# A state-space layer and a routed feed-forward on one core: the scan's sum as one bf16 product, and the round's steps moved to other chunks

## The chip, the core and the metric

The kernel runs on one NeuronCore of a Trainium2 chip. The core has a tensor engine (PE in the profile; its weight loads are listed apart as PEld), a vector engine (DVE), a scalar engine (ACT), GpSimd (POOL) and a sync engine (SP) that issues transfers. Each engine runs its own instructions in their program order and waits for the others by semaphores. The metric is the device time of the whole kernel in microseconds, lower is better. Before the change the median of three runs is 478.21 us (477.84 to 479.93).

## What is computed

A sequence of 4096 tokens with 256 values goes through two layers, each followed by adding its input and a layer norm. The first is a selective state-space layer, the second a feed-forward of eight experts, of which each token uses one:

```python
xz = input_tensor @ W_in                        # 256 -> 1024: conv_in, gated
y = causal_conv4(conv_in) + conv_b              # per channel, 512 channels
convolved = silu(y)
x_dbl = convolved @ W_x                         # 33 columns: delta, B (16), C (16)
delta = softplus(x_dbl[..., :1])
h = exp(delta * A) * h + delta * B * convolved[..., :16]     # step by step, 16 states
ssm_out = sum(h * C, axis=-1)                   # one number per token
out = (ssm_out + convolved * D_param) * silu(gated) @ W_out
x = layernorm(x + out)
expert_idx = argmax(x @ Wr.T + br)
x = layernorm(x + relu(x @ W1[e].T + b1[e]) @ W2[e].T + b2[e])   # e = expert_idx
```

## The kernel before

**Rounds and chunks.** The first layer works on blocks of 512 tokens (TB), eight of them (NB). A loop over k = 0 to 7 is one round per block. In a round the tensor engine makes the eight chunks of the input projection, `project(k, 0)` to `project(k, 7)`; each is a product of 128 channels by 512 tokens in fp32 (an fp32 matmul shows as two records). Between the chunks stand steps of earlier blocks: a = k - 1, b = k - 2, c = k - 3. The tensor engine's order is the order of these calls, written out by hand (`manual_schedule`). The other engines' orders are made when the program is built, from the same dependences, and are fixed from then on.

**The steps of a block**, in the order in which a block passes through them:

- `project` evicts each chunk on ACT; `taps` (L723 in the profile) adds the other three convolution taps on DVE, three operations of 128x512 per chunk of channels.
- `gauge` multiplies by W_x; `gauge_out` turns the result so that tokens lie on partitions; a chain of small DVE operations (L810 to L837) with one exponential on ACT forms the step sizes and writes them with B and C into `sr`.
- `scan` turns `sr` back (matmuls on tile pt, L846), takes an exponential (tile dA, ACT), runs the recurrence with one DVE scan over 512 tokens (tile h, L852), and multiplies by C (tile hC, L860).
- `gate` sums hC over the 16 states with matmuls against ones (tile py, L872), adds the skip path on DVE (tile cv, L879) and multiplies by the gate: three of four channel groups on POOL and one on DVE (tile sg, L884).
- `look` and `look_out` compute the router's product on the block's input (tiles prx, rx, pf, rparts) and add it beside the block's rows in xb.
- `project_out(i, j)` for j = 0 to 3 multiplies 128 tokens by W_out (tile po, L920; DVE adds the rows, L924, and takes the norm's statistics); at j = 3 ACT writes the normed rows x1 (L940), which SP stores to DRAM.
- `choose` finds the expert of each token on DVE (tiles lg, best, oh). `rank` counts tokens per expert with small matmuls (tile pr), and makes row and column marks: colh on DVE, rowh on POOL. `place` multiplies these (tile pz) and adds the result to `lists` on DVE (L1023).
- `blocks_of(i)` builds, after blocks 2, 4, 5 and 7, a table of which expert's weights the next blocks of 128 tokens need (`table`) and starts the weights' gathers on POOL. `tokens_of(i)` then reads the token numbers out of `lists` with a matmul (tile pi, L445), and POOL gathers the rows (tile xg, L504).

**The experts.** `expert(n)` runs n quarters of the second layer's blocks: `turn`, `hidden` twice, `close` twice, `finish`. From round 6 on, quarters stand between the chunks (`fill`); after the loop the last blocks' steps stand between quarters, and the remaining experts follow to the end.

**Buffers.** The tile pools have two buffers for xb and xTb, three for cv, sg and acc. In PSUM there are three banks for projection chunks (tag mm), three for po, py and pe (tag o) and two for all small products (tag tr: px, prx, pz, pxo, pr, pt, pf, pn, pi). The two last serve in turn, so each product in tag tr needs the eviction of the second last.

**The router behind the projection.** `router_behind` folds the router's weights into eight columns beside W_out (matmuls on tile pwo, L490, with eight columns each), half of it in round 1 and half in round 2.

In one round (k) before, the calls stand as follows, with P0 to P7 for the chunks:

```
P0  gate(b)  P1  gauge(a)  P2  tokens_of(c-1)  P3  gauge_out(a)  po(b,0)
P4  rank(c)  po(b,1)  P5  blocks_of(c)  look(k)  po(b,2)  P6  look_out(a)  scan(a)
po(b,3)  choose(b)  P7  place(c)
```

Of the kernel before, what the change touches and what calls it, by code (L numbers as in the profile page):

```python
# [47 lines left out]
P = 128  # L48
# [51 lines left out]
def mamba_moe(  # L100
# [27 lines left out]
    def bank(tag, name, bufs=None):  # L128
        return ps.tile([P, 512], F32, tag=tag, name=name, bufs=bufs)
# [111 lines left out]

    sr = const.tile([P, JT, NR], F32, name="sr")
    nc.gpsimd.memset(sr, 0.0)
    ones8 = const.tile([P, NE], F32, name="ones8")
    nc.gpsimd.memset(ones8, 1.0)

# [223 lines left out]
    def router_weights():  # L470
# [9 lines left out]
            wr[:, :, 0:NE], wr[:, :, 0:NE], mean.unsqueeze(1).to_broadcast([P, DC, NE]),  # L480
            ALU.subtract,
        )

    def router_behind(half):
        po = bank("tr", f"pwo{half}", 2)
        pov = po[:, 0 : CC * NE].rearrange("p (c e) -> p c e", e=NE)
        cs = slice(half * CC // 2, (half + 1) * CC // 2)
        for c in range(CC)[cs]:
            for dc in range(DC):
                nc.tensor.matmul(  # L490
                    pov[:, c, :], lhsT=woutT[:, dc, c * P : (c + 1) * P], rhs=wr[:, dc, 0:NE],
                    start=(dc == 0), stop=(dc == DC - 1),
                )
        nc.scalar.copy(wout[:, cs, D : D + NE], pov[:, cs, :])


    xgs, wes, turned, hid, last, open_, ys = {}, {}, {}, {}, {}, {}, {}
# [343 lines left out]
    def scan(i):  # L841
        s_, cv = st[i], st[i]["cv"]
        hbefore = st[i - 1]["h"] if i else None
        pt = bank("tr", f"pt{i}", 2)
        for j in range(JT):
            nc.tensor.transpose(pt[0:NR, j * P : (j + 1) * P], sr[:, j, :], ident)  # L846
        dA = a2.tile([NS, TB], F32, tag="dA", name=f"dA{i}", bufs=1)
        nc.scalar.activation(dA, pt[RD : RD + NS, :], AF.Exp, scale=nega)
        dBx = a2.tile([NS, TB], F32, tag="dBx", name=f"dBx{i}", bufs=1)
        nc.vector.tensor_tensor(dBx, pt[RB : RB + NS, :], cv[0:NS, 0, :], ALU.mult)  # L850
        h = a2.tile([NS, TB], F32, tag="h", name=f"h{i}")
        nc.vector.tensor_tensor_scan(  # L852
            h, dA, dBx, 0.0 if hbefore is None else hbefore[:, TB - 1 : TB],
            ALU.mult, ALU.add,
        )

        hC = a2.tile([Q + NS, TB // 2], F32, tag="hC", name=f"hC{i}", bufs=1)
        for g in range(2):
            at = slice(g * TB // 2, (g + 1) * TB // 2)
            nc.vector.tensor_tensor(  # L860
                hC[g * Q : g * Q + NS, :], pt[RC : RC + NS, at], h[:, at], ALU.mult
            )
        s_["h"], s_["hC"] = h, hC

    def gate(i):
        cv, sg = st[i]["cv"], st[i]["sg"]


        pys = [bank("o", f"py{i}_{g}") for g in range(2)]
        for g, py in enumerate(pys):  # L870
            at = slice(g * Q, g * Q + NS)
            nc.tensor.matmul(  # L872
                py[:, 0 : TB // 2], lhsT=ones[at, :], rhs=st[i]["hC"][at, :], start=True,
                stop=True, tile_position=(g * Q, 0),
            )
        for c in range(CC):
            for g, py in enumerate(pys):
                at = slice(g * TB // 2, (g + 1) * TB // 2)
                nc.vector.scalar_tensor_tensor(  # L879
                    cv[:, c, at], cv[:, c, at], dp[:, c : c + 1], py[:, 0 : TB // 2],  # L880
                    ALU.mult, ALU.add,
                )
            eng = nc.vector if c == CC - 1 or (c % 2 and i >= NB - 2) else nc.gpsimd
            eng.tensor_tensor(sg[:, c, :], cv[:, c, :], sg[:, c, :], ALU.mult)  # L884

    def look(i):

        prx = bank("tr", f"prx{i}", 2)
        n = TB // 2
        for dc in range(DC):  # L890
            for h in range(2):
                g = (2 * dc + h) * Q
                nc.tensor.matmul(
                    prx[g : g + Q, 0:n], lhsT=wr[:, dc, :],
                    rhs=st[i]["xTb"][:, dc, h * n : (h + 1) * n], start=True, stop=True,
                    tile_position=(0, g),
                )
        st[i]["rx"] = a2.tile([P, n], F32, tag="rx", name=f"rx{i}")
        nc.scalar.copy(st[i]["rx"], prx[:, 0:n])

    def look_out(i):

        pf = bank("tr", f"pf{i}", 2)
        for s in range(2):
            at = slice(s * P, (s + 1) * P)
            nc.tensor.transpose(pf[:, at], st[i]["rx"][:, at], ident)

        pfv = pf[:, 0 : 2 * P].rearrange("p (s c h e) -> p s c h e", s=2, c=DC, h=2)
        beside = st[i]["xb"][:, :, D : D + NE].rearrange("p (h s) e -> p h s e", s=2)
        parts = a2.tile([P, 2, DC, 2, NE], F32, tag="rparts", name=f"rparts{i}", bufs=1)  # L910
        for s in range(2):
            nc.scalar.copy(parts[:, s], pfv[:, s, :, :, 0:NE])
# [134 lines left out]
    for k in range(NB):  # L1047
        if have(k + 1):
            load(k + 1)
        if k == 0:  # L1050
            load_later()
            load_rows(0)
        if have(k + 1):
            load_rows(k + 1)
        a, b, c = k - 1, k - 2, k - 3

        fill = {NB - 2: (0, 0, 0, 0, 0, 0, 2, 2), NB - 1: (1, 1, 2, 1, 1, 1, 1, 1)}.get(k, (0,) * 8)
        project(k, 0)
        if k == 2:
            router_behind(1)  # L1060
        if have(b):
            gate(b)
        expert(fill[0])
        project(k, 1)
        if have(a):
            gauge(a)
        expert(fill[1])
        project(k, 2)
        if k == 0:
            router_weights()  # L1070
        if have(c - 1):
            tokens_of(c - 1)
        expert(fill[2])
        project(k, 3)
        if have(a):
            gauge_out(a)

        taps(k, CC - 1)
        if have(b):
            project_out(b, 0)  # L1080
        expert(fill[3])
        project(k, 4)
        if k == 1:
            router_behind(0)
        if have(c):
            rank(c)
        if have(b):
            project_out(b, 1)
        expert(fill[4])
        project(k, 5)  # L1090
        if have(c):
            blocks_of(c)
        look(k)
        if have(b):
            project_out(b, 2)
        expert(fill[5])
        project(k, 6)
        if have(a):
            look_out(a)
            scan(a)  # L1100
        if k == NB - 2:

            turn(0)
        if have(b):
            project_out(b, 3)
            choose(b)
        expert(fill[6])
        project(k, 7)
        if have(c):
            place(c)  # L1110
        expert(fill[7])
    a, b, c = NB - 1, NB - 2, NB - 3
    gate(b)
    gauge(a)
    expert(2)
    tokens_of(c - 1)
    gauge_out(a)
    expert(2)
    project_out(b, 0)
    expert()  # L1120
    rank(c)
    project_out(b, 1)
    expert()
    blocks_of(c)
    project_out(b, 2)
    expert()
    look_out(a)
    scan(a)
    expert()
    project_out(b, 3)  # L1130
    choose(b)
# [75 lines left out]
```

## Time and profile before

| | us |
|---|---|
| median of three runs | 478.21 |
| the profiled execution | 479.7 |
| its span, first to last instruction | 478.0 |
| tensor engine busy | 466.2 |
| DVE busy | 340.4 |
| ACT busy | 223.4 |
| POOL busy | 185.5 |
| mean granted clock of the tensor engine | 0.993 |

The profile is one execution. Its views used below are: busy time by engine; a timeline, which lists instructions of one engine in order of time with start, duration, line, operation, tiles and count, and in brackets the idle time just before, with what ended it; and a table of stretches, which gives busy time of each engine and the granted clock of the tensor engine in chosen stretches of the span. Matmuls are pipelined, and the shown end of one lies beyond the start of the next, so their cost is read from start to start. A duration in DVE's timeline also contains the time in which an instruction is held before it can read.

The loop's rounds take the span's first half. From about 290 us on the tensor engine has little but experts, and DVE is busy for about half of the time.

### The profile page before, as it was taken

The page shows a single profiled execution, that of the slowest core. Times are in us where ns is not written, and L with a number is a line of the kernel's source. Part 1 is how long each engine was busy: PE and PEld are TensorE (multiplying, and loading weights), DVE is VectorE, ACT ScalarE, POOL GpSimd, SP SyncE. Part 2 cuts the span into 40 slices and gives each one's busy share as a digit, 9 for nine tenths or more (in the row PEclk, how much of TensorE's full clock was granted, in tenths as well). Part 3 has the DMA queues.
Part 4 walks back from the last instruction along what each step waited for, and adds up shares of the span by engine and source line. Part 5 has one row for each costly group of instructions (what it writes and reads, how often), then busy time and mean ns, then how long its engine had stood idle before and what let it go on. Part 6 is the DMA issues. An engine that isn't in the chain of part 4 may idle for free. (4 is left out here: it accounts for less than half of the span.)

```text
span 478.0 us, 7559 instructions
## 1 busy us (share of the span) xinstructions
PE 466.2 (98%) x2606; PEld 350.1 (73%) x2606; DVE 340.4 (71%) x1120; ACT 223.4 (47%) x453; POOL 185.5 (39%) x194
## 2 busy tenths in 40 slices
PE   8999999999999999999999999999999999999994
PEld 6444554645455566677788999999989898989884
DVE  1687959899898997986998978755446565645453
ACT  3776767886896877584625131212212121212111
POOL 2001203442418372450433423435445456654541
PEclk9998999999999999999999999999999999999998
DMA  8401012040124945250766759799997279977910
GB/s 237 166 1 45 0 42 91 1 132 0 47 87 149 431 159 188 110 199 18 271 242 225 270 209 366 260 368 350 359 347 277 60 253 345 313 247 245 353 44 22
DMA packets 23401, 89.98 MB, mean 188 GB/s; under 512 B 4914, under 2 KB 14909, under 8 KB 19650
## 3 DMA queue, kind: packets, MB, share of 16 engines
q0 software_dynamic: 8752, 74.71, 42.7%
q1 hardware_dynamic: 13650, 14.50, 9.3%
q8 instruction: 21, 0.34, 0.3%
q10 hardware_dynamic: 960, 0.27, 0.3%
q14 instruction: 18, 0.15, 0.1%
HBM read 87.78 MB, written 9.43 MB: 203 GB/s over the span
## 5 line engine op out<-in xcount | busy, mean ns | idle before, releaser
L744 PE MATMUL pm<-xTb,win 128*128 128x512 f32 (+1 forms) x264 | 122.5, 598 | 0.0
L587 PEld LDWEIGHTS ph<-xgT,we 128*128 128x128 f32 x864 | 100.8, 192 | 5.5 <-DVE r L637 1.3
L587 PE MATMUL ph<-xgT,we 128*128 128x128 f32 x864 | 103.0, 276 | 0.0
L612 PE MATMUL pe<-we,hT 128*128 128x256 f32 x432 | 98.9, 380 | 0.0
L612 PEld LDWEIGHTS pe<-we,hT 128*128 128x128 f32 x432 | 79.7, 190 | 10.0 <-DVE lg L960 0.3
L723 DVE SCALAR_TENSOR_TENSOR acc<-xc,cw,acc 128x512 f32<-128x512 f32 x96 | 72.6, 777 | 15.7 <-DMA wx<-in_W_x 8.6
L744 PEld LDWEIGHTS pm<-xTb,win 128*128 128x128 f32 x264 | 49.2, 195 | 45.5 <-issue 40.8
L262 ACT ACTIVATE sdm<-mvm,eps 128x1 f32<-128x1 f32 x32 | 9.4, 294 | 122.6 <-DVE mvm L260 116.8
L522 POOL DMA_INDIRECT we<-in_experts,widx x32 | 33.6, 1049 | 85.0 <-DVE r L637 24.9
L920 PE MATMUL po<-wout,sg 128*128 128x264 f32 x256 | 64.1, 392 | 1.0 <-DVE sg L884 0.9
L884 POOL TENSOR_TENSOR sg<-cv,sg 128x512 f32<-128x512 f32 x22 | 32.7, 1492 | 59.6 <-DVE cv L879 46.1
L920 PEld LDWEIGHTS po<-wout,sg 128*128 128x128 f32 x256 | 46.1, 190 | 11.0 <-issue 2.9
L650 POOL DMA_INDIRECT out<-y,tidx x32 | 32.9, 1027 | 38.5 <-DVE y L264 30.5
L598 DVE TENSOR_SCALAR hT<-ph,we 128x128 f32<-128x128 f32 x108 | 31.3, 341 | 20.7 <-PE ph L587 20.6
L637 DVE TENSOR_TENSOR r<-pe,xs 128x256 f32<-128x256 f32 x32 | 13.5, 422 | 43.9 <-PE pe L612 43.8
L504 POOL DMA_INDIRECT xg<-x1d,tidx x32 | 31.9, 998 | 29.7 <-DVE xd L810 7.5
L596 ACT ACTIVATE hT<-ph,we 128x128 f32<-128x128 f32 x108 | 30.8, 368 | 23.2 <-PE ph L587 20.7
L1008 POOL TENSOR_SCALAR rowh<-lrow,row,code 128x256 f16<-128x256 bf16 x20 | 26.0, 1307 | 27.9 <-DVE row L1000 26.7
L879 DVE SCALAR_TENSOR_TENSOR cv<-cv,dp,py 128x256 f32<-128x256 f32 x64 | 28.5, 469 | 3.4 <-PE py L872 3.4
L759 ACT ACTIVATE sg<-pm 128x512 f32<-128x512 f32 x32 | 19.1, 596 | 19.5 <-PE pm L744 17.0
L761 ACT COPY xc<-pm 128x512 f32<-128x512 f32 x32 | 18.6, 582 | 19.1 <-PE pm L744 18.8
L763 ACT ACTIVATE acc<-pm,cb,cw 128x512 f32<-128x512 f32 x32 | 25.1, 784 | 0.0
(219 smaller groups left out, 604.4 us busy)
## 6 DMA issues: line engine op xcount, KB each, us to landing
xb<-in_x SPq DMA_DIRECT2D x8, 512.0 KB, 6.1
x1d<-x SPq DMA_DIRECT2D x8, 512.0 KB, 4.8
xTb<-in_xT SPq DMA_DIRECT2D x7, 512.0 KB, 3.3
win<-in_W_in SPq DMA_DIRECT2D x1, 512.0 KB, 5.2
we<-in_W_outT SPq DMA_DIRECT2D x1, 512.0 KB, 5.9
wout<-in_W_out SPq DMA_DIRECT2D x1, 512.0 KB, 6.9
we<-in_experts,widx POOLq DMA_INDIRECT x32, 10.3
xg<-x1d,tidx POOLq DMA_INDIRECT x32, 6.6
```

The costliest lines, as they stand in the source:

```text
L504: nc.gpsimd.indirect_dma_start(out=to, out_offset=None, in_=x1d[0:rows, :], in_offset=bass.IndirectOffsetOnAxis(ap=at, axis=0),)
L522: nc.gpsimd.indirect_dma_start(out=wes[n][:, :], out_offset=None, in_=experts, in_offset=bass.IndirectOffsetOnAxis(ap=weights[n], axis=0), ...
L587: nc.tensor.matmul(ph[:, n * w : (n + 1) * w], lhsT=we[:, at : at + P], rhs=xgT[:, dc * w : (dc + 1) * w], start=(dc == 0), stop=(dc == DC ...
L596: nc.scalar.activation(hT[:, fc, :], ph[:, n * w : (n + 1) * w], AF.Relu, bias=bias)
L598: last[b] = nc.vector.tensor_scalar(hT[:, fc, :], ph[:, n * w : (n + 1) * w], bias, 0.0, ALU.add, ALU.max)
L612: nc.tensor.matmul(py[:, 0:D], lhsT=hT[:, fc, 0:P], rhs=out_weights(fc), start=(fc == 0), stop=(fc == FC - 1),)
L650: moved = nc.gpsimd.indirect_dma_start(out=out, out_offset=bass.IndirectOffsetOnAxis(ap=at, axis=0), in_=rows, in_offset=None, bounds_chec ...
L723: nc.vector.scalar_tensor_tensor(acc, xc[:, c, k : k + TB], cw[:, c, k : k + 1], acc, ALU.mult, ALU.add)
L744: nc.tensor.matmul(banks[c][:, at], lhsT=win[:, dc, c * P : (c + 1) * P], rhs=xTb[:, dc, at], start=(dc == 0), stop=(dc == DC - 1),)
L879: nc.vector.scalar_tensor_tensor(cv[:, c, at], cv[:, c, at], dp[:, c : c + 1], py[:, 0 : TB // 2], ALU.mult, ALU.add,)
L884: eng.tensor_tensor(sg[:, c, :], cv[:, c, :], sg[:, c, :], ALU.mult)
L920: nc.tensor.matmul(po[:, 0 : D + NE], lhsT=sg[:, c, j * P : (j + 1) * P], rhs=wout[:, c, :], start=(c == 0), stop=(c == CC - 1),)
```

## The change

**The sum.** `scan` writes h times C into a fp32 tile `parts_` of 128 rows (16 used), then two more groups of 16 rows, each the rest that is left of the group before when its upper 16 bits are taken away. The upper 16 bits of an fp32 number are a bf16 number, so the three groups' upper halves sum to the fp32 value. `gate` multiplies these halves, read in place with a step of two elements, by ones in bf16: one matmul of 512 columns into one bank, in place of two fp32 products of 256 columns. The skip path's DVE operations then cover 512 columns each: four in place of eight. The unused rows are zeroed once at the start.

**The router.** `router_behind` is gone. `look("w")` and `look_out("w")` in round 1 do the same product on W_out's transpose with the code that the blocks use.

**The round.** `load_rows` moves from the block's predecessor's round to the round after the block's own, behind c's last `project_out`. The calls of a round now stand so:

```
P0  po(c,2)  P1  po(c,3)  choose(c)  load_rows(a)  gauge(a)  look(k)
P2  gate(b)  place(c-1)  P3  gauge_out(a)  P4  tokens_of(c-1)  P5  P6  rank(c)
po(b,0)  P7  po(b,1)  blocks_of(c)  scan(a)  look_out(a)
```

In the last round (k = 7) rank(c), blocks_of(c) and place(c) stand behind P4, P5 and P7. The experts' first two quarters come at the end of round 6 (four before), with `turn(0)` just ahead of them, and round 7 has ten (nine before). After the loop the steps left of blocks 5, 6 and 7 are put between quarters in the same manner.

```diff
-        hC = a2.tile([Q + NS, TB // 2], F32, tag="hC", name=f"hC{i}", bufs=1)
-        for g in range(2):
-            at = slice(g * TB // 2, (g + 1) * TB // 2)
+        s_["h"] = h
+        nc.vector.tensor_tensor(parts_[0:NS, :], pt[RC : RC + NS, :], h, ALU.mult)
+        for n in range(2):
+            this = slice(n * Q, n * Q + NS)
             nc.vector.tensor_tensor(
-                hC[g * Q : g * Q + NS, :], pt[RC : RC + NS, at], h[:, at], ALU.mult
-            )
-        s_["h"], s_["hC"] = h, hC
+                parts_[(n + 1) * Q : (n + 1) * Q + NS, :], parts_[this, :], upper(this),
+                ALU.subtract,
+            )
+
+    def upper(rows):
+
+        return parts_[rows, :].bitcast(BF16).rearrange("p (t two) -> p t two", two=2)[:, :, 1]
...
-        pys = [bank("o", f"py{i}_{g}") for g in range(2)]
-        for g, py in enumerate(pys):
-            at = slice(g * Q, g * Q + NS)
-            nc.tensor.matmul(
-                py[:, 0 : TB // 2], lhsT=ones[at, :], rhs=st[i]["hC"][at, :], start=True,
-                stop=True, tile_position=(g * Q, 0),
-            )
+        py = bank("o", f"py{i}")
+        nc.tensor.matmul(py, lhsT=oneb, rhs=upper(slice(0, P)), start=True, stop=True)
         for c in range(CC):
-            for g, py in enumerate(pys):
-                at = slice(g * TB // 2, (g + 1) * TB // 2)
-                nc.vector.scalar_tensor_tensor(
-                    cv[:, c, at], cv[:, c, at], dp[:, c : c + 1], py[:, 0 : TB // 2],
-                    ALU.mult, ALU.add,
-                )
+            nc.vector.scalar_tensor_tensor(
+                cv[:, c, :], cv[:, c, :], dp[:, c : c + 1], py, ALU.mult, ALU.add
+            )
             eng = nc.vector if c == CC - 1 or (c % 2 and i >= NB - 2) else nc.gpsimd
             eng.tensor_tensor(sg[:, c, :], cv[:, c, :], sg[:, c, :], ALU.mult)
```

The loop after the change (its calls alone; `project_out` is po above):

```python
        fill = {NB - 2: (0, 0, 0, 0, 0, 0, 0, 2), NB - 1: (2, 1, 2, 1, 1, 1, 1, 1)}.get(k, (0,) * 8)
        soon = k == NB - 1
        project(k, 0)
        if have(c):
            project_out(c, JT - 2)
        expert(fill[0])
        project(k, 1)
        if have(c):
            project_out(c, JT - 1)
            choose(c)
        if have(a):
            load_rows(a)
            gauge(a)
            look(k)
        expert(fill[1])
        project(k, 2)
        if have(b):
            gate(b)
...
        if have(c - 1):
            place(c - 1)
        expert(fill[2])
        project(k, 3)
        if have(a):
            gauge_out(a)

        taps(k, CC - 1)
        expert(fill[3])
        project(k, 4)
        if have(c - 1):
            tokens_of(c - 1)
...
        project(k, 6)
        if have(c) and not soon:
            rank(c)
        if have(b):
            project_out(b, 0)
        expert(fill[6])
        project(k, 7)
        if have(b):
            project_out(b, 1)
        if have(c):
            if soon:
                place(c)
            else:
                blocks_of(c)
        if have(a):
            scan(a)
            look_out(a)
        if fill[7] and not soon:

            turn(0)
        expert(fill[7])
```

## The prediction

> **What bounds the kernel now.** I read the page's first two parts, then the tensor engine's timeline from end to end, then the vector engine's for one round, and last the granted clock by stretches.
>
> ```profile
> PE 466.2 (98%) x2606; PEld 350.1 (73%) x2606; DVE 340.4 (71%) x1120; ACT 223.4 (47%) x453; POOL 185.5 (39%) x194
> PEclk9998999999999999999999999999999999999998
> ```
>
> The tensor engine is full from 4 to 470 us, so time goes where matmuls are removed or holes open between them. The shares hide how near the vector engine (DVE) is. One round of the old order, tensor engine first:
>
> ```profile
> 70.79 1.06 PE L872 MATMUL py<-hC,ones 16*128 16x256 f32 x4
> 71.79 1.98 PE L744 MATMUL pm<-xTb,win 128*128 128x512 f32 x4
> ...
> 91.01 0.38 PE L906 MATMUL pf<-ident,rx 128*128 128x128 f32 x2
> 91.28 0.61 PE L846 MATMUL pt<-ident,sr 128*80 128x128 f32 x4
> ...
> 97.54 0.70 PE L872 MATMUL py<-hC,ones 16*128 16x256 f32 x4
> 98.17 1.99 PE L744 MATMUL pm<-xTb,win 128*128 128x512 f32 x4
> ```
> ```profile
> 74.18 0.87 DVE L960 TENSOR_TENSOR lg<-lg,brb 128x32 f32<-128x32 f32 x1
> 74.98 1.80 DVE L723 SCALAR_TENSOR_TENSOR acc<-xc,cw,acc 128x512 f32<-128x512 f32 x1
> ...
> 90.90 0.24 DVE L837 TENSOR_TENSOR sr<-xd,sr 128x64 f32<-128x64 f32 x1
> ```
> ```profile
> 72.48 3.76 POOL L884 TENSOR_TENSOR sg<-cv,sg 128x512 f32<-128x512 f32 x3 [18.09 <-DVE cv L879]
> ```
>
> The reader is to see a loop through two engines. The scan's transposes pt read sr; DVE finished sr at 91.14, 0.14 us before pt began. From the gate (70.79) to pt the tensor engine has 20.5 us of work and DVE needs 20.35: a tie. In the next rounds sr is ready at 118.28, 145.05 and 170.77 for pt at 118.83, 145.93 and 172.71. So DVE is a second bound, hidden by 0.1 to 1.9 us. Rounds from pt to pt: 26.2, 27.55, 27.1, 26.8.
>
> **What the change takes off the tensor engine.** [...] Folding the router by look("w") costs 0.57 + 0.27 in place of 0.81 + 0.96: 0.9. The half clock goes too:
>
> ```profile
> 41.39:44.80 3.41, 3.22 (x16) 2.03 (x15) 3.01 (x6) 2.35 (x5) 0.00 (x0) 1.00 0.43 156
> 44.80:48.21 3.41, 3.41 (x8) 0.78 (x8) 3.41 (x6) 0.82 (x2) 2.35 (x2) 0.50 0.01 2
> ```
>
> (Columns: stretch, sum, busy PE, PEld, DVE, ACT, POOL, clock, DMA.) After a stretch with 8-column and 16-row matmuls and holes of 0.67 and 0.19 nearby, one window of 3.41 us ran at half clock: 1.7 us. Both narrow groups leave that place. Holes of 0.95 (105.9), 0.41 (141.1), 0.63 (173.3) and 0.26 (234.9) could go as well.
>
> **DVE's own work** hardly changes. Eight cv operations at a step of 0.39 become four of about 0.66 (256 more elements cost 0.27, from the 128x512 step of 0.66 at L723): -0.5. Two hC at 0.45 become three 16x512 operations at 0.61 to 0.7 (from dBx, 0.61): +1.0. The router's additions, the larger memset and ScalarE's copies lie beside full engines at the start and cost nothing on the path.
>
> **What the re-timing does** is decisive. In the new round the tensor engine goes pt 0.45, pf 0.27, P0 1.8, po 1.8, P1 1.75, po 1.8, gauge 1.9, look 0.57, P2 1.75, gate: 12.1 us from pt to gate (6.3 before), and from gate to pt 0.25 + place 0.44 + P3 to P7 8.7 + pxo 0.44 + rank 0.15 + two po 3.6 = 13.6 (20.5 before). In the built order DVE still has between gate and sr, in one queue: cv 2.64, choice 1.4 (its last three steps now stand alone), taps acc2 and acc3 6 x 0.66 = 3.96, sg 0.61, lists 0.34, xd, e and delta 0.36, ranking and colh 1.5 (five dependent steps of 0.18, as at 171.71 to 172.61, then 0.6), xb and sta 0.68, the chain s to sr 2.57 (168.20 to 170.77, where it stands alone), and 0.72 from gate to first cv (97.54 to 98.27; one pass in place of two, same latency). Sum 14.8. Added to it is the time in which GpSimd blocks DVE. The lines at 74.18 and 74.98 took 0.87 and 1.80 where their like take 0.18 and 0.74: each ended with one of GpSimd's three products. Per round that cost 1.4 to 2.5 us.
>
> [...] With cv in whole rows, the first three cv follow in 2 us, so GpSimd's three products (1.27 each) run back to back for 3.8 us; cv itself passes. [...] I take 2.4 (the round at 97.54 showed 2.5). So **sr comes 17.2 us after the gate where the tensor engine arrives after 13.6**. A smaller stall at P6 (its bank waits for ScalarE, behind the four x1 rows) lies inside this.
>
> On the other leg DVE is in time: after pt, dA comes 2.6 us later and the scan's end at 4.4, then parts and taps 3.95 and 3.5 more = 11.9 against 12.1. The loop is therefore 12.1 + 17.2 = **29.3 us**, 28.9 at k=3 with no place.
>
> **Where pt stands, before and after.** pt(0): 38.07, 39.3 (sr is released by gauge_out, which look and look("w") put back by 1.2). pt(1): 65.05, 63.7 (clock, router and gate won, DVE again late by some 0.7). pt(2): 91.28, 92.6. pt(3): 118.83, 121.9. pt(4): 145.93, 151.2.
>
> **The first lookup**, k=6:
>
> ```profile
> 158.42 0.51 PE L445 MATMUL pi<-pick,lists 128*128 128x5 f32 x4
> ```
> ```profile
> 166.43 1.48 POOL L504 DMA_INDIRECT xg<-x1d,tidx  x1 [5.68 <-DVE xd L810]
> ```
> ```profile
> 173.93 0.41 PE L555 MATMUL pg<-ident,xg 128*128 128x128 f32 x2 [0.63 <-DMA xg<-x1d,tidx]
> ```
>
> Before, lists was complete a round's start earlier. Now place(2) stands right behind the gate of the same round and pi two chunks on; lists, which pi reads, is added by DVE only 9.5 us after the gate (behind cv, taps and choice), while the tensor engine is at pi after 4.7. It waits 4.9 us, and P5, P6, rank, po, P7 and po are queued behind it. pt comes 19.1 after the gate. tidx is ready at 12.6, the rows land 7.5 later (166.43 to 173.93) at 20.1, when turn(0) is due: no second hole. turn(0): 151.2 + 12.3 + 20.3 = 183.8, against 173.93: +9.9.
>
> [...] I take 1.3.
>
> After turn(0) both orders have equal work: po and experts fill the wait (in round 7 the tensor engine has 12 quarters of about 1.8 us more, so DVE falls off the path). The remaining three gates give 3 x 0.4 and one hole 0.26: -1.5. SP's row loads now wait for ScalarE's x1 in the same round, 6.5 us after the gate, and land (6.1 us) long before the 20 us later use. Sum: 9.9 + 1.3 - 1.5 = +9.7. Profiled execution 479.7 + 9.7 = 489.4; the median of runs stands 1.5 under the profiled one, so **487.9**.
>
> **Rivals.** *The tensor engine's work decides* (0.11): if DVE's chain after the gate took under 13.6 us, the savings count in full: 3.8 + 0.9 + 1.7 + about 2.5 of holes = 8.9, time 469.3. For it: 98% busy. Against it: the tie at 91.14, which the new order tightens. *The two cancel* (0.11): a loop of 26.9 instead of 29.3 in four rounds, for instance if GpSimd blocks nothing, gives 478.5. *Half clock in every round* (0.18): each round's 3.6 us hole with the thin transposes after it drops the clock in three more windows, 5.1 us: 493. The forecast itself has 0.60, own range 482 to 491.
>
> About 0.5% (2.4 us) is what a measurement can tell from no change. Faster 0.11, same 0.10, slower 0.79. The range 479 to 494 leaves out the first rival and little above.
>
> **What would show it.** DVE's last sr operation ending just before pt in every round with the tensor engine idle 2 to 4 us in front of pt (or P6); pt to pt about 29; pi waiting for lists some 5 us; a clock of 0.5 after it; gate about 0.25; cv about 0.74 long; GpSimd's products back to back. A round of 26.3 with no hole before pt would refute it.

## The result and the profile after

The changed kernel takes **506.75 us** (505.35 to 507.45, four runs) against 478.02 (477.81 to 479.93): 1.0588 times as long, 95% interval 1.0551 to 1.0625. It is slower, as forecast, but by 28.7 us where 9.7 were forecast, and outside the range. The profiled execution took 507.28 us with a span of 505.6.

The page of the changed kernel, first part and the row of the granted clock:

```profile
PE 470.9 (93%) x2576; PEld 351.2 (69%) x2576; DVE 353.7 (70%) x1097; ACT 213.5 (42%) x446; POOL 185.0 (37%) x195
PEclk9999999898998989999999799999999999999998
```

The tensor engine fell from 98% to 93%, and its clock now has dips in five places in place of one. One round, the first lookup and one place near 284 us, from the tensor engine's timeline of the changed kernel (start, duration, instruction, in brackets the idle time ahead of it and what ended that):

```profile
122.83 1.04 PE L837 MATMUL pt<-ident,sr 128*80 128x128 f32 x4 [2.44 <-DVE sr L828]
...
124.09 2.82 PE L735 MATMUL pm<-xTb,win 128*128 128x512 f32 x4
...
136.38 0.39 PE L866 MATMUL py<-parts__144,oneb 128*128 128x512 bf16 x1
136.61 0.61 PE L1013 MATMUL pz<-colh,rowh 128*128 128x128 f16 x8
...
153.54 1.04 PE L837 MATMUL pt<-ident,sr 128*80 128x128 f32 x4 [2.44 <-DVE sr L828]
...
176.04 0.61 PE L448 MATMUL pi<-pick,lists 128*128 128x5 f32 x4 [4.19 <-DVE lists L1017]
...
188.93 0.44 PE L546 MATMUL pg<-ident,xg 128*128 128x128 f32 x2 [0.69 <-ACT rparts L906]
...
283.85 6.67 PE L578 MATMUL ph<-xgT,we 128*128 128x128 f32 x32 [3.76 <-DVE xgT L558]
```

The gate (py) is 0.23 us ahead of its successor, as forecast. But 2.44 to 2.46 us of idle stand ahead of pt in three rounds running, and the projection behind it takes 2.82 us where a projection takes 1.98: half clock (granted 0.50 for 3.41 us from 91.84, 122.56 and 153.28). From gate to pt there are now 17.16 us, from pt to the next gate 13.55; the round is 30.71 us long, against 26.2 to 27.6 before. Of the 3.6 us that the tensor engine was to wait on the way from gate to pt, 3.0 came (0.58 of them ahead of a projection and of the small products pr). pi waits 4.19 us, turn(0) stands at 188.93 (173.93 before), and behind it a second large hole appears where the kernel before had none: the 32 products ph after it take 6.67 us in place of some 3.8 (granted 0.50 from 282.99 to 289.82).

GpSimd and DVE behind a gate of the changed kernel, first GpSimd's timeline, then DVE's:

```profile
137.64 4.28 POOL L872 TENSOR_TENSOR sg<-cv,sg 128x512 f32<-128x512 f32 x3 [13.81 <-DVE cv L868]
```
```profile
138.22 0.72 DVE L868 SCALAR_TENSOR_TENSOR cv<-cv,dp,py 128x512 f32<-128x512 f32 x1
...
139.03 1.76 DVE L714 SCALAR_TENSOR_TENSOR acc<-xc,cw,acc 128x512 f32<-128x512 f32 x1
140.71 1.25 DVE L954 TENSOR_TENSOR lg<-lg,brb 128x32 f32<-128x32 f32 x1
```

The three products run back to back for 4.28 us. In that time cv, which reads PSUM, keeps its 0.72, and the first two operations with both inputs in SBUF take 1.76 and 1.25 where their like take 0.74 and 0.18.

So the loss has two halves: 15.0 us up to turn(0), and 12.6 from there to the last matmul (310.4 us against 297.8).

### The profile page after: what moved, and what is told of

It is laid out like the page before. It is cut to its first block, busy times and chain, and to the rows that moved or that the text cites. A ratio compares the mean times of both kernels' runs of the same rounds, so it can differ in the third digit from the quotient of the medians.

```text
span 505.6 us, 7469 instructions
## 1 busy us (share of the span) xinstructions
PE 470.9 (93%) x2576; PEld 351.2 (69%) x2576; DVE 353.7 (70%) x1097; ACT 213.5 (42%) x446; POOL 185.0 (37%) x195
## 5 line engine op out<-in xcount | busy, mean ns | idle before, releaser
L735 PE MATMUL pm<-xTb,win 128*128 128x512 f32 (+1 forms) x264 | 125.1, 609 | 2.0 <-ACT acc L754 0.9
L578 PE MATMUL ph<-xgT,we 128*128 128x128 f32 x864 | 106.4, 281 | 4.9 <-DVE xgT L558 4.9
L578 PEld LDWEIGHTS ph<-xgT,we 128*128 128x128 f32 x864 | 103.5, 196 | 10.4 <-DVE xgT L558 5.7
L714 DVE SCALAR_TENSOR_TENSOR acc<-xc,cw,acc 128x512 f32<-128x512 f32 x96 | 76.8, 810 | 22.2 <-ACT acc L754 21.5
L914 PEld LDWEIGHTS po<-wout,sg 128*128 128x128 f32 x256 | 47.8, 190 | 16.3 <-issue 8.6
L868 DVE SCALAR_TENSOR_TENSOR cv<-cv,dp,py 128x512 f32<-128x512 f32 x32 | 22.9, 737 | 2.8 <-PE py L866 2.8
```

Source lines behind the costliest of these rows:

```text
L578: nc.tensor.matmul(ph[:, n * w : (n + 1) * w], lhsT=we[:, at : at + P], rhs=xgT[:, dc * w : (dc + 1) * w], start=(dc == 0), stop=(dc == DC ...
L714: nc.vector.scalar_tensor_tensor(acc, xc[:, c, k : k + TB], cw[:, c, k : k + 1], acc, ALU.mult, ALU.add)
L735: nc.tensor.matmul(banks[c][:, at], lhsT=win[:, dc, c * P : (c + 1) * P], rhs=xTb[:, dc, at], start=(dc == 0), stop=(dc == DC - 1),)
L914: nc.tensor.matmul(po[:, 0 : D + NE], lhsT=sg[:, c, j * P : (j + 1) * P], rhs=wout[:, c, :], start=(c == 0), stop=(c == CC - 1),)
```

## The experiments

No kernel leaves out any of the work. The batches differ in level: in those of e1 to e8 and of e16 the kernel before itself took 483.6 to 484.8 us in place of 477 to 478, and their traces show waits of up to 2.5 us ahead of expert products (pe) between 415 and 472 us, which the other traces don't have. The profile names no releaser for the longest of them; late expert weights are a guess. So the time is compared as a ratio to the kernel before in the same batch, and the place of a gain by marks inside the trace, ahead of those waits: pt(4), turn(0), and the stretch from turn(0) to turn(19).

| kernel | time, us | before, us | ratio, 95% | pt(4) | turn(0) | turn(0) to turn(19) |
|---|---|---|---|---|---|---|
| before | 478.02 | | 1 | 145.93 | 173.93 | 188.97 |
| after | 506.75 | 478.02 | 1.0588 [1.0551, 1.0625] | 153.54 | 188.93 | 201.73 |
| e1 sum alone | 489.23 | 484.75 | 1.0102 [1.0057, 1.0147] | 149.13 | 177.75 | 189.86 |
| e2 sum, router | 490.71 | 484.75 | 1.0117 [1.0056, 1.0179] | 148.24 | 176.86 | 189.85 |
| e3 round, router | 508.98 | 484.75 | 1.0466 [1.0391, 1.0540] | 149.41 | 185.26 | 200.47 |
| e4 one quarter more | 510.18 | 484.75 | 1.0507 [1.0457, 1.0556] | 152.54 | 188.72 | 199.02 |
| e5 products on DVE | 505.22 | 484.01 | 1.0433 [1.0369, 1.0497] | 144.96 | 180.03 | 202.17 |
| e6 filler | 511.45 | 484.01 | 1.0548 [1.0488, 1.0607] | 150.78 | 188.07 | 200.51 |
| e7 place early | 515.10 | 484.01 | 1.0629 [1.0564, 1.0693] | 154.79 | 188.30 | 204.18 |
| e8 gate early | 510.02 | 484.01 | 1.0542 [1.0475, 1.0608] | 152.24 | 183.63 | 203.75 |
| e9 last gate later | 498.85 | 477.23 | 1.0446 [1.0404, 1.0488] | 153.79 | 189.25 | 194.32 |
| e10 router alone | 478.14 | 477.23 | 1.0008 [0.9984, 1.0032] | 144.90 | 172.76 | 188.99 |
| e11 old round, tuned | 493.44 | 477.23 | 1.0335 [1.0291, 1.0379] | 155.49 | 186.81 | 189.63 |
| e12 old tail | 494.45 | 477.23 | 1.0365 [1.0322, 1.0407] | 151.83 | 188.11 | 189.48 |
| e13 e12 + e5 | 486.50 | 478.38 | 1.0174 [1.0151, 1.0198] | 146.19 | 179.92 | 189.56 |
| e14 e13 + e7 | 485.19 | 478.38 | 1.0137 [1.0115, 1.0160] | 146.29 | 176.34 | 192.49 |
| e15 e14 + e8 | 488.12 | 478.38 | 1.0218 [1.0195, 1.0241] | 147.81 | 177.84 | 191.32 |
| e16 all together | 488.68 | 483.58 | 1.0102 [1.0051, 1.0153] | 145.88 | 177.11 | 188.52 |

### Which part of the change costs the time: e1, e2, e10, e3

e1 is the kernel before with the change's scan and gate functions and nothing else; e2 adds look("w") and look_out("w") in place of router_behind; e10 has this router alone; e3 is the change with the two functions of before.

> Round and router as before, only the state sum and the gate of the change. Theory T (the new order of the round causes the loss, the sum is harmless): the gate takes 0.22 us in place of 0.63, DVE gains about 0.5 us at cv and loses 1.0 at the three pieces, and the two nearly cancel: 474 to 478.5 us, rounds from pt to pt of 26.5 to 27.5. Rival R (the sum causes it: three dependent DVE operations and an operand read with a stride): gate late behind the pieces in every round, 485 us or more.

> Round as before, with the change's sum, gate and its way of folding the router. Theory T: as the sum alone, less 0.9 us of matmuls, and less 1.7 us if the half-clock window at 44.8 us goes with the narrow matmuls: 472 to 477 us, faster than before. Rival R: 485 us or more. A third outcome, same as the sum alone, would say that the router's place cost nothing.

> The kernel before with only the router's folding of the change. Theory T (narrow matmuls of the old folding cost 0.9 us and bring the half-clock window at 44.8 us): turn(0) 0.9 to 2.6 us earlier than 173.9, total 1 to 2.5 us under the kernel before. Rival (DVE sets the rounds, so time won on the tensor engine in round 1 and 2 is waited away): turn(0) within 0.5 us, no difference.

> Round and router of the change, with the sum and the gate of before. Theory T: the loop is still pt to gate on the tensor engine plus gate to sr on DVE; the gate adds 0.4 us and cv in eight pieces 0.5: rounds of 30 to 31.5 us, 503 to 512 us in all. Rival R: most of the loss goes, 478 to 490 us.

The sum alone makes the old round 1.0% slower (489.23 us stands against 484.75 in its batch). The theory missed; the rival named the right wait, but not a loss of this size: the sum is neither harmless nor the cause of 28 us. e2 came out as the sum alone, its third outcome, and e10 level with the kernel before, though both were expected to gain. The tensor engine's timeline of e1:

```profile
92.28 0.61 PE L848 MATMUL pt<-ident,sr 128*80 128x128 f32 x4
...
100.10 0.39 PE L877 MATMUL py<-parts__144,oneb 128*128 128x512 bf16 x1 [1.49 <-DVE parts__144 L863]
```

In the old round the gate stood 6.3 us after pt; the third piece is ready only 7.8 after it, and the tensor engine waits about 1.5 us or more in each of the first five rounds with a gate, four times what the shorter gate saves. This is what the re-timing gives room to: in the changed kernel 0.32 us stand ahead of the first gate and nothing ahead of the next five. But e3, the re-timing with the old sum, keeps most of the loss (1.0466): 11.3 of the 15.0 us at turn(0), and 11.5 of the 12.8 from there to turn(19). The rest comes with the sum in the new order too: e3's round from pt(2) to pt(3), at full clock, takes 28.75 us where the change without half clock takes 29.23 (e6 below). The router's folding gains 0.9 us (e2 against e1) and 1.2 us (e10) at turn(0), and the half-clock window near 44 us is gone in both (mean granted clock 0.996 and 0.998, against 0.993 before); in the time of the whole kernel e10 shows no difference. **Most of the loss is the new order's.**

### The rounds: e6, e5, e8

e6 fills the hole ahead of pt with products that nobody reads:

```diff
         pt = bank("tr", f"pt{i}", 2)
+        for _ in range(18 if 2 <= i <= 5 else 0):
+            nc.tensor.matmul(pt[:, 0 : LH * P], lhsT=oneb, rhs=lrow, start=True, stop=True)
         for j in range(JT):
```

> The change with 18 idle bf16 products of 256 columns (some 1.9 us) on the tensor engine in the hole ahead of pt in four rounds; what they write is overwritten by pt. Theory T (the half clock after pt is caused by the hole of 2.4 us): the windows at 92, 123 and 153 us go, pt to gate is 12.1 us in every round, pt(4) at 150.5 to 152 and the total 3 to 5 us under the change. Rival (the drop comes from the narrow transposes, or stands at fixed times): the windows stay, rounds stay at 30.7 us.

The tensor engine's timeline of e6:

```profile
118.93 2.13 PE L837 MATMUL pt<-lrow,oneb 128*128 128x256 bf16 x18
121.54 0.60 PE L839 MATMUL pt<-ident,sr 128*80 128x128 f32 x4 [0.48 <-DVE sr L828]
...
133.55 0.39 PE L868 MATMUL py<-parts__144,oneb 128*128 128x512 bf16 x1
```

The three half-clock windows in the rounds are gone (pt takes 0.60 us where the change has 1.04), pt to gate is 12.0 us, and the rounds from pt to pt are 29.23 and 29.24: what the forecast had without half clock. So half clock cost 1.5 us in each of the rounds that had it. Little of it reaches the end: pi now waits 4.58 us, and from pt(4) to turn(0) e6 takes 37.29 us where the change takes 35.39, so that turn(0) comes only 0.9 us earlier.

e5 takes the gate products from GpSimd:

```diff
-            eng = nc.vector if c == CC - 1 or (c % 2 and i >= NB - 2) else nc.gpsimd
-            eng.tensor_tensor(sg[:, c, :], cv[:, c, :], sg[:, c, :], ALU.mult)
+            nc.vector.tensor_tensor(sg[:, c, :], cv[:, c, :], sg[:, c, :], ALU.mult)
```

> The change with all four gate products on DVE, none on GpSimd. Theory T (GpSimd's three products block DVE for 2.4 us a round): DVE takes 3 x 0.68 = 2.0 us more work and loses the block, gate to pt 16.8 us in place of 17.2, rounds 0.3 to 0.5 us shorter, pt(4) 0.5 to 2 us earlier, the total 0 to 3 us under the change. Rival (GpSimd blocks DVE little, so the products cost DVE their whole length): gate to pt 18.5 us or more, rounds of 32 us, the total 5 to 10 us over the change.

The stretch from a gate to the next pt in both kernels (columns: stretch, length, then busy time and number of instructions of PE, PEld, DVE, ACT and POOL, clock, DMA share, GB/s), first the changed kernel, then e5, where the stretch begins 0.04 us ahead of the gate and ends 0.06 us ahead of pt:

```profile
136.38:153.54 17.16, 14.13 (x56) 7.72 (x55) 16.19 (x49) 14.78 (x24) 8.60 (x8) 0.99 0.29 93
```
```profile
129.40:144.90 15.50, 13.99 (x56) 7.78 (x54) 14.88 (x52) 14.54 (x25) 2.89 (x3) 1.00 0.33 103
```

And DVE's timeline of e5 at the place that was shown above:

```profile
132.03 0.68 DVE L871 TENSOR_TENSOR sg<-cv,sg 128x512 f32<-128x512 f32 x1
132.63 0.19 DVE L953 TENSOR_TENSOR lg<-lg,brb 128x32 f32<-128x32 f32 x1
132.73 0.75 DVE L714 SCALAR_TENSOR_TENSOR acc<-xc,cw,acc 128x512 f32<-128x512 f32 x1
```

DVE has three instructions more and is busy 1.31 us less; acc and lg are back at 0.75 and 0.19. With the three products at a step of 0.6 (132.03 to 132.63), DVE was held up, by this estimate, for 1.31 + 1.8 = 3.1 us by products that last 4.28. **On DVE the three products cost less than what their run on GpSimd cost DVE.** Rounds are 27.5 us, the hole ahead of pt is 1.4, no half clock follows (pt takes 0.61), and turn(0) comes 8.9 us earlier. The expectation had the sign, with 0.3 to 0.5 us a round where 1.6 came from DVE's leg and 1.6 from pt to gate, where the half clock had been.

e8 moves the gate ahead of look and the third projection:

```diff
             gauge(a)
+        if have(b):
+            gate(b)
+        if have(a):
             look(k)
         expert(fill[1])
         project(k, 2)
-        if have(b):
-            gate(b)
```

> The change with the gate moved ahead of look and the third projection, 2.3 us earlier after pt. Theory T (the loop is the tensor engine's leg from pt to gate plus DVE's from gate to sr): the first leg falls from 12.1 to 9.9 (where the third piece is ready), the second stays near 17.2, the hole ahead of pt shrinks or moves, rounds of 27 to 28 us, pt(4) at 146 to 149, total 6 to 12 us under the change. Rival (DVE's whole work in a round is the bound, so what leaves one leg turns up in the other): gate to pt grows to 18.5 us or more, rounds of 28.5 to 29.5, pt(4) at 150 to 153, total 0 to 4 us under the change.

The tensor engine's timeline of e8:

```profile
95.21 0.61 PE L837 MATMUL pt<-ident,sr 128*80 128x128 f32 x4 [1.16 <-DVE sr L828]
...
104.83 0.40 PE L866 MATMUL py<-parts__144,oneb 128*128 128x512 bf16 x1
...
115.72 1.98 PE L735 MATMUL pm<-xTb,win 128*128 128x512 f32 x4 [1.92 <-ACT acc L754]
...
123.73 0.61 PE L837 MATMUL pt<-ident,sr 128*80 128x128 f32 x4 [0.53 <-DVE sr L828]
```

Pt to gate falls to 9.6 us, and gate to pt grows to 18.9. The round is 28.5, 0.7 below that of e6, and most of the wait has moved to another place (1.92 ahead of a projection). The rival's numbers held: what leaves one leg turns up in the other, and the gate's place mostly shares the waiting out. That DVE's work alone is the bound is not shown: in this round it is busy for 26.1 of 28.5 us, and which of its own waits make up the rest stays open.

### The first lookup: e7

e7 places each chunk at the round's first projection, 9 us ahead of the gate:

```diff
         project(k, 0)
         if have(c):
             project_out(c, JT - 2)
+        if have(c - 1):
+            place(c - 1)
...
-        if have(c - 1):
-            place(c - 1)
         expert(fill[2])
```

> The change with the placing of each chunk moved from right behind the gate to the first projection of the round, 9 us ahead of the gate. Theory T (pi waits because lists is added behind the gate's work on DVE): the 4.2 us hole ahead of pi and the half-clock window behind it go, turn(0) at 182 to 185.5 us in place of 188.9, total 3 to 7 us under the change. Rival (the gathered rows land when they land, and a hole ahead of pg takes the place of the one ahead of pi): turn(0) at 188 or later, the total within 1.5 us of the change.

The tensor engine's timeline of e7:

```profile
172.92 0.51 PE L448 MATMUL pi<-pick,lists 128*128 128x5 f32 x4
...
186.78 0.61 PE L837 MATMUL pt<-ident,sr 128*80 128x128 f32 x4 [3.39 <-DVE sr L828]
...
188.30 0.44 PE L546 MATMUL pg<-ident,xg 128*128 128x128 f32 x2 [0.69 <-ACT rparts L906]
```

My theory fell, and not quite as the rival had it. The hole ahead of pi is gone, and one of 3.39 stands ahead of pt instead: behind lists, sr was nearly as late. Which of the two shows depends here on where place stands; turn(0) gains 0.6 us, and the rounds get 0.5 us longer. e8 bears on this too: with the gate earlier pi no longer waits, pt waits 1.89 us, and turn(0) comes 5.3 us earlier than in the change, 4.0 of them in this one round.

### Behind turn(0): e4, e9, e12

At 283.85 the turned rows (xgT) are late. DVE's timeline of the changed kernel shows why:

```profile
281.59 1.22 DVE L965 TENSOR_TENSOR earlier<-earlier,here 128x8 bf16<-128x8 bf16 x1
282.73 0.73 DVE L868 SCALAR_TENSOR_TENSOR cv<-cv,dp,py 128x512 f32<-128x512 f32 x1
283.39 0.41 DVE L558 COPY xgT<-pg 128x256 f32<-128x256 f32 x1
```

The turn was issued right behind the last gate, and its copy queues behind choice and all four cv on DVE (and behind GpSimd's block: `earlier`, 8 elements wide, takes 1.22 us where its like take 0.17, while a product of GpSimd runs from 281.03 to 282.78). In the kernel before 23 expert quarters stood ahead of that gate, now 22, so another quarter meets it. e4 adds a quarter in the eighth round, (2, 1, 2, 1, 1, 1, 1, 2); e9 moves the gate past one quarter:

```diff
     place(c)
-    expert()
-    gate(a)
     expert(2)
+    gate(a)
+    expert()
     tokens_of(c)
```

> The change with one expert quarter more in the last chunk's round, so that 23 quarters stand before the seventh gate, as in the kernel before, and not 22. Theory T (what is lost after the first turn comes from the phase of the quarters against the gate): the 3.8 us hole before ph near 284 us, the two half-clock windows behind it and the holes near 325 us go: 496 to 500 us, with turn(0) unmoved near 189 us. Rival (the loss after the first turn comes from the late start of the experts or their loads): 504 to 508 us, as the change.

> The change with the last gate one expert quarter later, so that the copy of the turned rows goes into DVE's queue ahead of the gate's work; the quarters' order against the lookups stays. Theory T (the hole of 3.8 us ahead of ph near 284 us is that copy queued behind the gate's cv): the hole and the two half-clock windows behind it go, from turn(0) to the end 5 to 8 us less. Rival (as with one quarter more, another wait of the same size takes its place, for instance for the gathered rows): within 2 us of the change.

With e4 that hole goes, but the quarter then runs ahead of its rows; the tensor engine's timeline of e4:

```profile
266.68 0.66 PE L546 MATMUL pg<-ident,xg 128*128 128x128 f32 x2 [4.53 <-DMA xg<-x1d,tidx]
```

So e4 gains only 2.7 us from turn(0) to turn(19). e9 leaves the quarters where they stand against the lookups. DVE's timeline of e9 has the copy ahead of the cv, and the tensor engine's has no hole ahead of ph:

```profile
278.45 0.42 DVE L558 COPY xgT<-pg 128x256 f32<-128x256 f32 x1
...
278.88 0.74 DVE L868 SCALAR_TENSOR_TENSOR cv<-cv,dp,py 128x512 f32<-128x512 f32 x1
```
```profile
279.61 3.82 PE L578 MATMUL ph<-xgT,we 128*128 128x128 f32 x32
```

Both half-clock windows go with the hole (ph takes 3.82 us in place of 6.67): 7.4 us.

e12 keeps the change up to the seventh round and orders the eighth and all behind it as before (its seventh round ends with two of its four products with wout still open; they are made at the first two projections of the eighth).

> The change up to the seventh chunk's round; the last round and the stretch behind it in the order of the kernel before. Theory T (what is lost after turn(0) comes from the new order of the work there: short waits where each step follows its source too closely, and the wrong quarter behind the last gate): from turn(0) to the last matmul 298 to 303 us in place of 310.4, total 8 to 12 us under the change. Rival (the loss is carried over from the rounds, as late rows, late lookups or DVE's backlog): 307 us or more, total within 3 us of the change.

All idle places of e12 in the tensor engine's timeline from turn(0) to 330 us:

```profile
188.11 0.44 PE L546 MATMUL pg<-ident,xg 128*128 128x128 f32 x2 [0.69 <-ACT rparts L906]
189.24 3.84 PE L578 MATMUL ph<-xgT,we 128*128 128x128 f32 x32 [0.69 <-DVE xgT L558]
...
249.44 0.66 PE L791 MATMUL pxo<-ident,pxs 128*128 128x128 f32 x4 [0.26 <-ACT codes L453]
250.84 1.56 PE L603 MATMUL pe<-we,hT 128*128 128x256 f32 x6 [0.30 <-DVE hT L589]
```

Behind turn(0) the kernel before has one idle place up to 330 us, and one more of 0.73 us at 446.68:

```profile
235.18 0.66 PE L800 MATMUL pxo<-ident,pxs 128*128 128x128 f32 x4 [0.26 <-ACT codes L450]
```

From turn(0) to the last matmul e12 takes 298.1 us, the kernel before 297.8, the change 310.4. The late start costs nothing later on; **the whole second half of the loss is the order of the work behind turn(0)**. In the trace of the change it is 9.2 us more idle time (10.2 against 1.0: 3.8 in the hole ahead of ph, the rest at ten hand-overs of 0.4 to 1.1, such as pxo and pf behind lists, pm behind ScalarE's hT, pe behind DVE's hT) and two half-clock windows (0.50 from 282.99 to 289.82), 3.4 us.

### Do the causes add up: e11, e13, e14, e15, e16

e11 asks whether the old round can carry the new sum: e2 with the gate one projection later and the products of chunks 0 to 5 on DVE. The others start from e12 with these products on DVE (e13), then place early (e14), then the gate early (e15).

> The kernel before with the sum, the gate and the router of the change, the gate one projection later, and the gate products of chunks 0 to 5 all on DVE. Theory T (DVE's round is the second bound, GpSimd's products block it for some 3.4 us a round against 2.0 that they cost on DVE, and the pieces are ready 7.9 us after pt, where the gate now stands): no hole ahead of py or pt over 0.5 us, rounds of 26 to 26.8 us, total 3 to 8 us under the kernel before. Rival (the pieces or ScalarE are late all the same): holes of 1 us or more in each round, total at the kernel before or over it.

> The change with the old tail and with the gate products of chunks 0 to 5 on DVE. Theory T (the causes add up): rounds of 27.5 us, the 4.3 us hole ahead of pi still there, turn(0) at 179.5 to 181, 298 us from there to the last matmul, total 7 to 9 us under the change with the old tail alone. Rival (the old tail was helped by the late start): over 300 us behind turn(0).

> As the kernel before it, with the placing at the first projection of the round. Theory T (pi's wait and DVE's late sr hid each other: each alone leaves the other in place): now both are relieved, no hole over 1.5 us ahead of pi, no double half-clock window there, turn(0) at 174 to 177 us. Rival (a third thing holds turn(0), the rows or DVE's table work): turn(0) at 179 or later.

> As the kernel before it, with the gate ahead of look and the third projection. Theory T (DVE's whole round is the bound, 27 us with the products on it, and the gate's place only moves waiting about): rounds within 0.5 us of the kernel before it, total within 2 us of it. Rival (the gate's place sets the loop): rounds down to the tensor engine's 26 us, turn(0) 4 us or more earlier, the total under the kernel before the change.

e11 is the largest miss. Its tensor engine's timeline:

```profile
104.04 0.39 PE L865 MATMUL py<-parts__144,oneb 128*128 128x512 bf16 x1
...
113.93 1.31 PE L913 MATMUL po<-wout,sg 128*128 128x264 f32 x4 [2.68 <-DVE sg L871]
...
124.99 0.60 PE L836 MATMUL pt<-ident,sr 128*80 128x128 f32 x4
```

The gate no longer waits, nor does pt, but the products with wout follow the gate too closely: on DVE, behind its other work, its last two sg come only 9 to 10 us after the gate, and po waits 2.68 us for them. So this order needs room behind the gate too, which the re-timing also gives. e11 moves the gate and the products at once; which of the two makes sg late was not separated.

e13 came out as the sum of e5 and e12: turn(0) at 179.92, 189.56 us on to turn(19). In e14 turn(0) moves to 176.34: with DVE relieved, the early placing is worth 3.6 us where alone it was worth 0.6. So the two waits had hidden each other. It did not go wholly as expected, as the tensor engine's timeline of e14 shows:

```profile
162.98 0.50 PE L448 MATMUL pi<-pick,lists 128*128 128x5 f32 x4
...
174.82 0.61 PE L837 MATMUL pt<-ident,sr 128*80 128x128 f32 x4 [1.17 <-DVE sr L828]
...
176.34 0.44 PE L546 MATMUL pg<-ident,xg 128*128 128x128 f32 x2 [0.69 <-ACT rparts L906]
177.46 6.76 PE L578 MATMUL ph<-xgT,we 128*128 128x128 f32 x32 [0.69 <-DVE xgT L558]
```

No single hole is long, but three follow closely (1.17, 0.69 and 0.69 us), and ph behind them takes 6.76 us in place of 3.84: 2.92 us more, by my estimate over one window of half clock (1.7). They do not all lie within one window of 3.41 us, as I then put it in the expectation of e16: from the start of the first to the end of the last are 3.81 us (173.65 to 177.46). e15 has rounds of 27.5 us against 28.0, and turn(0) 1.5 us later: no gain, as the theory had it, though its median is 2.9 us higher, not within 2. Its profiled execution took 485.78 us, one of the two shortest of six, so the trace doesn't show where the median loses.

e16 places early in the seventh round alone, and puts two products with wout of that round around turn(0):

```diff
         if fill[7] and not soon:
+            project_out(b, 2)
             turn(0)
+            project_out(b, 3)
+            choose(b)
```

> The kernel with old tail, products on DVE and early placing, but the early placing in the seventh round alone (elsewhere it added 0.45 us a round), and the last two products with wout of that round on either side of turn(0) in place of a round later, so that its two holes of 0.7 us are filled. Theory T (holes of 1.2 + 0.7 + 0.7 us within one window bring the two half-clock windows behind turn(0)): no half clock there, 4 to 6 us under e14, 479 to 481.5 us, level with the kernel before or up to 0.7% over it. Rival (the drop has another cause, or the two products only move a wait): over 483 us.

The tensor engine's timeline of e16:

```profile
174.66 0.61 PE L837 MATMUL pt<-ident,sr 128*80 128x128 f32 x4 [1.22 <-DVE sr L828]
...
180.66 3.84 PE L578 MATMUL ph<-xgT,we 128*128 128x128 f32 x32 [1.39 <-DVE xgT L558]
```

The half clock is gone (ph takes 3.84 us) and turn(19) comes 3.2 us earlier than in e14, at 365.63: 2.7 us behind the kernel before (362.90). The ratio is 1.0102 with an interval of 1.0051 to 1.0153, in a batch with the late waits ahead of pe (one of 2.43 us in this trace); the lower end of the interval agrees with the 0.7% expected, the middle does not. No version was faster than the kernel before; the nearest, the router alone, is level with it.

## Why the prediction was right in sign and wrong in size

By the profiled executions the loss is 27.6 us where the sum had 9.7. Of the 17.9 missing, 14.1 are one step and 3.8 another.

- **"After turn(0) both orders have equal work ... so DVE falls off the path" (-1.5) is the step that failed.** It measured +12.6. The work is equal, but the time isn't set by work alone: each hand-over needs its source ready, and the new order put steps right behind their sources. I counted matmuls and quarters, and did not go through DVE's queue at the gates behind turn(0), where one quarter of phase puts the copy of the turned rows behind four cv. e12 and e9 show it.
- **Half clock, taken once (1.3 us), came in four windows before turn(0)** (0.50 for 3.41 us from 91.84, 122.56, 153.28 and 177.18), three more than the sum had: some 5.1 us at 1.7 each (e6 measured 1.5 in a round), the price that the third rival named. With the smaller terms (the wait of pi 0.7 us shorter, pt(1) 0.6 earlier), that gives 15.0 us at turn(0) against 9.9 + 1.3. No run shows the 1.3: it was my estimate for one window, at the first lookup, where 1.7 came. The trace of before had full clock behind a hole of 0.95 us; of longer ones I had none to go by. Holes of 2.44 us sufficed, and the three windows that followed them I had left to a rival with a chance of 0.18.
- **The loop of 29.3 us was right**: 29.23 and 29.24 where e6 takes the half clock away, 28.98 in the round without place (28.9 forecast). Of its legs, 17.16 came for 17.2 and 12.0 for 12.1. But it was right as a sum, not as a model: e8 shows that the two legs are not fixed, and the 17.2 us were in part luck, as two of its terms were wrong against each other (next point).
- **GpSimd's block**, 2.4 us in the sum, near the 2.5 of one round of before, is 3.1 by e5. The products ran back to back as forecast, for 4.28 us in place of 3.8; cv passed (0.72 us; before the change 0.47 at 101.79, within a product of GpSimd from 101.09 to 102.90), and operations with two SBUF inputs waited (acc 1.76 us for 0.74, lg 1.25 for 0.18). I took the block 0.7 us too short, and had the other work on DVE about as much too long.
- **The first lookup**: the wait of pi 4.19 for 4.9, pt 20.3 us after the gate for 19.1 plus a half-clock window. The time was right; that the wait of pi is what holds the lookup was not (e7): sr was as late.
- **Gate, cv, router**: 0.23 for 0.25 (no row of before shows the 0.25, nor the 0.4 that each gate was to save; by the runs a gate went from 0.63 to 0.23); cv 0.737 us for 0.74; the router 0.9 to 1.2 at turn(0) for 0.9, without a measurable gain in the end. (One reading was off without effect: the hole of 0.95 us before the change stood at 107.4 us; 105.9 is where the row ahead of it begins.)

## What to carry to other kernels

When work is re-timed, go through the other engine's queue at every place where the order changes, the tail too, not only in the loop: an equal amount of work in a new order took 12.6 us longer here. Where two waits lie near each other, taking one away shows the other; change both before concluding that neither matters (0.6 us alone, 3.6 once DVE was relieved). A second engine that computes beside DVE is worth its place only if DVE doesn't wait for it: here DVE lost 3.1 us to save 1.8.

## What the hardware showed that I had not expected

Up to 500 us of the changed kernel's trace the granted clock goes to 0.50 at 91.84, 122.56, 153.28, 177.18 and 282.99 us and back to 1.00 at 95.26, 125.98, 156.70, 180.59 and 289.82. All ten times stand whole multiples of 3.41 us apart, and what went with the drops was the tensor engine's idle time in the 3.41 us ahead of each, not the length of a hole: 2.18, 2.18, 2.18, 2.28 and 2.90 us. Behind 1.91 us, the first part of the wait of pi (170.35 to 173.76), the clock stayed full. In e3 and e4 one window each with 2.5 us of idle (115.87 to 119.29, 118.93 to 122.34) was followed by half clock, and one each with 1.66 (from 88.57) and 1.62 (from 88.21) by full clock. The kernel before has, up to 470 us, one drop of another kind, at 44.80, behind 0.19 us of idle and eight of the old router's 8-column products; its cause stays open. Two windows, of the changed kernel (busy PE 1.23) and of e4 (1.79), each with the one that follows; columns as above:

```profile
88.43:91.84 3.41, 1.23 (x6) 0.72 (x4) 3.03 (x15) 3.38 (x4) 3.41 (x3) 1.00 0.46 154
91.84:95.26 3.42, 3.14 (x9) 2.07 (x10) 2.44 (x7) 1.05 (x4) 1.27 (x2) 0.50 0.00 0
```
```profile
88.21:91.62 3.41, 1.79 (x9) 1.18 (x7) 3.12 (x13) 3.35 (x6) 3.38 (x3) 1.00 0.46 154
91.62:95.03 3.41, 2.56 (x11) 1.63 (x12) 2.77 (x9) 1.61 (x4) 1.84 (x2) 1.00 0.00 0
```

Nearly the same hole ahead of pt (2.46 and 2.47 us) lies with 2.18 us in one window in the first, and is split into 1.62 and 0.85 in the second; the clock drops only in the first. Of the changed kernel's half-clock windows, one with 0.86 us of idle (282.99 to 286.41) was followed by another, and the five others, with 0.28 at most, by full clock; so one hole cost 1.7 us there or 3.4, by an estimate from 3.41 us at 0.50. A bf16 product over 512 columns whose moving operand takes every second 16-bit element took 0.23 us to the next start, near half of the 0.43 of one record of a 512-column fp32 product (four take 1.72, 128.53 to 130.25). So no large price of the stride was seen; the same product without a stride is in no trace here.
